# Whole-array products that may run as four 32-column products, chosen by a shortest path

## The chip, the cores and the metric

The kernel runs on one core of one Trainium2 chip. The metric is the time of one execution on the device in microseconds (us); three runs of the kernel before are known. One more view is the profile of a single execution: for every engine the start and duration of each instruction.

The core has five engines that run beside each other: TensorE (PE in the profile; its weight loads are listed apart as PEld), VectorE (DVE), ScalarE (ACT), GpSimd (POOL) and SyncE (SP). They synchronise through semaphores, and each works off its own instructions in order.

## The reference

Four graph layers run one after the other on `x` (32 batches of 512 nodes with 256 features) with one adjacency matrix; after each one the sum with the input is normalised. All is float32.

```python
# --- layer 0: attention of 8 heads of 32, two norms, a two-layer MLP ---
x = _layernorm(x + _L0_gnn_ref(x, adj, ...), axis=-1)
# --- layer 1: scores s1[n] + s2[m], leaky relu, masked softmax, times h = x W ---
x = _layernorm(x + _L1_gnn_ref(x, L1_gnn_W, L1_gnn_a, adj), axis=-1)
# --- layer 2: scores (x W1)(x W2)^T, leaky relu, masked softmax, times x W3, relu ---
x = _layernorm(x + _L2_gnn_ref(x, adj, L2_gnn_W1, L2_gnn_W2, L2_gnn_W3), axis=-1)
# --- layer 3: 4 heads of 64, scores as in layer 1 per head, elu ---
x = _layernorm(x + _L3_gnn_ref(x, adj, L3_gnn_W, L3_gnn_a), axis=-1)
```

Every matrix product of these lines is TensorE's work, and so are the transposes between them.

## The kernel before

The kernel is a recorder. `graph(b)` walks through the four layers for one batch and, instead of issuing instructions, calls `plan(engine, ns, run, reads, writes, ...)` for every piece of work: an engine, an estimated duration, a function that will issue the instructions, and the buffers read and written. The estimates in `ns` serve the planner alone.

`Plan.place` then puts the pieces of all 32 batches in one order. It keeps up to six batches in flight (`WAYS`), follows due times that come from one batch planned alone and from the tables `TENTHS`, `FIRST` and `LAST`, and hands out buffers and PSUM banks. In the order in which it places them, the pieces' `run` functions are called, and so each engine's instruction order is fixed when the program is built. One batch enters about every 82 us (`PACE` is 81.87).

Each TensorE piece has a number `tiling`, the shape in which the array works for it:

- 0: the whole array of 128 rows and 128 columns. All projections (`project_t`, L915, and `project`, L929), the MLP (L1136, L1148), the scores of layer 2 (L1244), the products with the attention of layers 1 and 2 (L1221, L1260), and the transposes (L902, L985, L1017, L1182).
- 1: 32 rows by 128 columns, four products beside each other. The scores of layer 0 (`exps`, L1034).
- 2: 128 rows by 32 columns, four beside each other. The product with the attention of layer 0 (L1093) and the sums of the softmax (L1065, L1281).
- 3: 128 rows by 64 columns, two beside each other. The product with the attention of layer 3 (L1306).

The planner adds `SWITCH` (100 ns) to TensorE's time where the shape changes (L590); the extra due time for a change, `STAY`, is 0, so shapes do not otherwise steer the order.

In the trace a float32 product is two passes, each one weight load and one matmul record; a transpose is one. A "whole product" of 512 columns in L915, L1136 or L1244 is two accumulated matmuls, four records; one of 256 or 257 columns in L929, L1148, L1221 or L1260 is four, eight records. A group of L1034 or L1093 is four matmuls, eight records.

Of the kernel before, what the change touches and what calls it, by code (L numbers as in the profile page):

```python
# [17 lines left out]
P = 128  # L18
# [419 lines left out]
PE, DVE, ACT, POOL, SP, DMA = "PE", "DVE", "ACT", "POOL", "SP", "DMA"  # L438
SIGNAL = 70
SWITCH = 100  # L440


class Slot:
# [6 lines left out]


class Op:
    def __init__(self, engine, ns, run, graph, rank, port, lag, tiling):
        self.engine, self.ns, self.run, self.graph, self.rank = engine, ns, run, graph, rank
        self.port, self.lag, self.tiling = port, lag, tiling
        self.then, self.missing, self.slots, self.ready = [], 0, [], 0.0


class Plan:
# [16 lines left out]

        self.graph, self.rank, self.start = graph, 0, start

    def __call__(self, engine, ns, run, reads=(), writes=(), port=False, lag=0, tiling=0):
        op = Op(engine, ns, run, self.graph, self.rank, port, lag, tiling)  # L480
        if not op.rank:
            op.ready = self.start
        self.rank += 1
        needs = {}
        for is_write, group in ((False, reads), (True, writes)):
            for item in group:
                slot, part = (item[0], item[1:]) if isinstance(item, tuple) else (item, None)
# [12 lines left out]
                if is_write:  # L500
                    if part is None:
                        parts.clear()
                    parts[part] = [op, []]
                else:
                    parts.setdefault(part, [None, []])[1].append(op)
        needs.pop(id(op), None)
        for other in needs.values():
            other.then.append(op)
        op.missing = len(needs)
        self.ops.append(op)  # L510
        return op
# [7 lines left out]
                live[slot.kind][r] += 1  # L519
        return live  # L520

    def place(self, urgency, ways, stay=0.0, early=1e12, run=True):

# [35 lines left out]
        while todo:  # L559
# [62 lines left out]
                del todo[op.graph]  # L622
                order.remove(op.graph)
            self.trace.append((t, op))
            if run and op.run:
                op.run()
        return end


def fast_path(  # L630
# [84 lines left out]
    def keep(name, shape, dtype=FP):  # L715

        slot = Slot(None)
        slot.tile = const.tile(shape, dtype, name=name)
        return slot

    def T(slot):
        return slot.tile if slot.kind is None else buffers[slot.kind][slot.index]
# [186 lines left out]
    def project_t(w, col, xT, dst, k):  # L909

        bank = Slot("bank")

        def run():
            for i in range(KC):
                nc.tensor.matmul(T(bank), T(w)[:, i, col:col + P], T(xT)[:, i, :],  # L915
                                 start=(i == 0), stop=(i == KC - 1))
        plan(PE, 1720, run, [w, xT], [bank])
        evac(dst, lambda t: t[:, k, :], bank, lambda b: b, N, [(dst, k)])

    def project(xT, w, col, width, dst):  # L920

        per = N // width
        for c0 in range(0, NC, per):
            bank = Slot("bank")

            def run(bank=bank, c0=c0):
                for j in range(per):
                    for k in range(KC):
                        nc.tensor.matmul(T(bank)[:, j * width:(j + 1) * width],  # L929
                                         T(xT)[:, k, (c0 + j) * P:(c0 + j + 1) * P],  # L930
                                         T(w)[:, k, col:col + width],
                                         start=(k == 0), stop=(k == KC - 1))
            plan(PE, per * KC * width * 1.69, run, [w, xT], [bank])
# [119 lines left out]
    def layer0(xs, at_once):  # L1053
# [77 lines left out]
        for d in range(KC):  # L1131
            bank = Slot("bank")

            def run(bank=bank, d=d):
                for k in range(KC):
                    nc.tensor.matmul(T(bank), T(w1_sb)[:, k, d * P:(d + 1) * P], T(nT)[:, k, :],  # L1136
                                     start=(k == 0), stop=(k == KC - 1))
            plan(PE, 1720, run, [w1_sb, nT], [bank])
            act(690, lambda bank=bank, d=d: nc.scalar.activation(
                T(hT)[:, d, :], T(bank), AF.Relu, bias=T(b1_sb)[:, d:d + 1]), [bank, b1_sb], [(hT, d)])  # L1140
        f = Slot("y")
        for c0 in range(0, NC, 2):
            bank = Slot("bank")

            def run(bank=bank, c0=c0):
                for j in range(2):
                    for k in range(KC):
                        nc.tensor.matmul(T(bank)[:, j * C:(j + 1) * C],  # L1148
                                         T(hT)[:, k, (c0 + j) * P:(c0 + j + 1) * P],
                                         T(w2_sb)[:, k, :], start=(k == 0), stop=(k == KC - 1))  # L1150
            plan(PE, 1730, run, [w2_sb, hT], [bank])
# [52 lines left out]
    def layer1(xs):  # L1204
# [11 lines left out]
        for c in range(NC):  # L1216
            bank, rinv = Slot("bank"), Slot("rs")

            def run(bank=bank, c=c):
                for m in range(NC):  # L1220
                    nc.tensor.matmul(T(bank)[:, :C + 1], T(p)[:, m, c * P:(c + 1) * P],  # L1221
                                     T(v)[:, m, 2:C + 3], start=(m == 0), stop=(m == NC - 1))
            plan(PE, 1740, run, [p, v], [bank])

            def out(bank=bank, c=c, rinv=rinv):
                nc.vector.reciprocal(T(rinv)[:, 0:1], T(bank)[:, C:C + 1])
                nc.vector.scalar_tensor_tensor(T(y)[:, c, :], T(bank)[:, :C], T(rinv)[:, 0:1],
                                               T(xs)[:, c, :], ALU.mult, ALU.add)
            dve(660, out, [bank, (xs, c)], [(y, c), rinv])
        return y  # L1230

    def layer2(xs):
# [6 lines left out]
        for m in range(NC):  # L1239
            bank, lo, es = Slot("bank"), Slot("e"), Slot("e")  # L1240

            def run(bank=bank, m=m):
                for k in range(KC):
                    nc.tensor.matmul(T(bank), T(xT)[:, k, m * P:(m + 1) * P], T(qT)[:, k, :],  # L1244
                                     start=(k == 0), stop=(k == KC - 1))
            plan(PE, 1720, run, [qT, xT], [bank])
# [8 lines left out]
        for c in range(NC):  # L1255
            bank = Slot("bank")

            def run(bank=bank, c=c):
                for m in range(NC):
                    nc.tensor.matmul(T(bank)[:, :C + 1], T(p)[:, m, c * P:(c + 1) * P],  # L1260
                                     T(v)[:, m, :C + 1], start=(m == 0), stop=(m == NC - 1))
            plan(PE, 1740, run, [p, v], [bank])
# [10 lines left out]
    def layer3(xs, at_once):  # L1273
# [9 lines left out]
        for k in range(KC):  # L1283
            av = Slot("bank")
            for m0 in range(0, NC, 2):
# [72 lines left out]


    graph(0)  # L1360
    alone = plan.place(lambda op: op.rank, 1, run=False)
    when = {op.rank: 10 * t / alone for t, op in plan.trace}

    def due(b, rank):
# [72 lines left out]
```

## Time and profile before

| | us |
|---|---|
| three runs | 2894.71, 2900.61, 2900.12 |
| median | 2900.12 |
| the profiled execution, first to last instruction (span) | 2891.7 |

The span leaves out what lies around the program's instructions, so it is a little shorter than the times. What costs most on TensorE, by line and form (busy time, mean of one record):

| line | shape | moving columns | records | busy us | mean ns |
|---|---|---|---|---|---|
| L1034 | 32 rows | 512 | 2048 | 302.6 | 644 |
| L1093 | 32 columns | 512 | 2048 | 275.2 | 609 |
| L1306 | 64 columns | 512 | 1024 | 242.8 | 605 |
| L915 (layer 0) | whole | 512 | 512 | 241.6 | 595 |
| L1221 | whole | 257 | 1024 | 237.8 | 381 |
| L1260 | whole | 257 | 1024 | 227.4 | 380 |
| L1244 | whole | 512 | 512 | 225.1 | 592 |
| L1148 | whole | 256 | 512 | 126.7 | 391 |
| L1136 | whole | 512 | 256 | 125.6 | 615 |

How to read it: matmul records overlap,[...] and their ends are modelled. The mean of one record is therefore not what it adds to the time. What a product adds is read as the distance between starts: from the first record of a group to the first record of the next. In a timeline line the first number is the start in us, the second the time to the end of the last record merged into that line; then come engine, source line, what is written and read, the array's rows and columns in use, the moving operand, and how many records were merged. In a windows line each engine's busy time follows the stretch, in the order PE, PEld, DVE, ACT, POOL, with the number of instructions, then the granted share of TensorE's clock, the share of the DMA engines and GB/s.

### The profile page before, as it was taken

The page shows a single profiled execution, that of the slowest core. Times are in us where ns is not written, and L with a number is a line of the kernel's source. Part 1 is how long each engine was busy: PE and PEld are TensorE (multiplying, and loading weights), DVE is VectorE, ACT ScalarE, POOL GpSimd, SP SyncE. Part 2 cuts the span into 40 slices and gives each one's busy share as a digit, 9 for nine tenths or more (in the row PEclk, how much of TensorE's full clock was granted, in tenths as well). Part 3 has the DMA queues.
Part 4 walks back from the last instruction along what each step waited for, and adds up shares of the span by engine and source line. Part 5 has one row for each costly group of instructions (what it writes and reads, how often), then busy time and mean ns, then how long its engine had stood idle before and what let it go on. Part 6 is the DMA issues. An engine that isn't in the chain of part 4 may idle for free.

```text
span 2891.7 us, 39629 instructions
## 1 busy us (share of the span) xinstructions
PE 2832.4 (98%) x14014; PEld 1579.2 (55%) x14014; DVE 2443.2 (84%) x4076; ACT 1885.5 (65%) x4104; POOL 865.9 (30%) x962
## 2 busy tenths in 40 slices
PE   8899999999999999999999999999999999999996
PEld 3355555555555555555555555555555555554562
DVE  5568888888888988888988888988888888888877
ACT  4566667666667666666666666666676666676553
POOL 1233333232333232332232333232333323333312
PEclk9999999999999999999999999999999999999998
DMA  6856777777777777777777777776776777775125
GB/s 168 169 110 142 150 159 164 154 144 160 145 161 153 159 149 158 149 160 157 147 152 150 157 157 155 152 160 144 162 157 150 155 153 146 161 163 115 35 55 132
DMA packets 101149, 424.44 MB, mean 147 GB/s; under 512 B 10256, under 2 KB 46224, under 8 KB 59152
## 3 DMA queue, kind: packets, MB, share of 16 engines
q0 software_dynamic: 49600, 325.08, 57.2%
q1 hardware_dynamic: 51344, 96.75, 11.6%
q8 instruction: 113, 1.85, 0.2%
q14 instruction: 92, 0.75, 0.1%
HBM read 63.38 MB, written 17.10 MB: 28 GB/s over the span
## 4 chain that ended last, share of the span: by engine, by line
PE 92%; DVE 3%; DMA 2%; issue 1%; ACT 1%; POOL 0%; SPq 0%; ACTq 0%; DVEq 0%; POOLq 0%
PE bank L929 15%; PE bank L915 11%; PE bank L1034 9%; PE bank L1093 8%; PE bank L1306 8%; PE bank L1221 7%; PE bank L1244 7%; PE bank L1260 7%; PE bank L902 5%; PE bank L1136 4%; PE bank L1148 4%; PE bank L1017 2%; DMA p<-p 1%; PE bank L1281 1%; PE bank L1065 1%
## 5 line engine op out<-in xcount | busy, mean ns | idle before, releaser
L972 POOL DMA_DIRECT2D p<-p x372 | 322.3, 871 | 1787.8 <-DMA p<-p 568.4
L1086 DVE TENSOR_TENSOR p<-p,edge_t 128x2048 f32<-128x2048 f32 x256 | 618.2, 2424 | 59.7 <-ACT p L1038 59.5
L890 ACT ACTIVATE t<-bank 128x512 f32<-128x512 f32 x640 | 373.5, 596 | 384.2 <-PE bank L915 125.4
L1038 ACT ACTIVATE p<-bank 128x512 f32<-128x512 f32 x1024 | 537.9, 599 | 89.2 <-PE bank L1034 87.6
L943 DVE BATCH_NORM_STATS2 st<-y 128x6 f32<-128x256 f32 x768 | 315.9, 411 | 35.6 <-POOL y L960 26.0
L1290 DVE TENSOR_SCALAR p<-p,e,e 128x512 f32<-128x512 f32 x512 | 331.3, 680 | 1.0 <-DMA p<-row 1.0
L960 POOL TENSOR_TENSOR y<-y,x 128x512 f32<-128x512 f32 x192 | 273.7, 1432 | 158.2 <-ACT y L1265 100.1
L1297 DVE TENSOR_TENSOR p<-p,edge_t 128x2048 f32<-128x2048 f32 x128 | 304.9, 2382 | 2.2
L1034 PE MATMUL bank<-t,t 32*128 32x512 f32 x2048 | 302.6, 644 | 0.0
L953 ACT ACTIVATE x<-y,rs,rs 128x256 f32<-128x256 f32 x512 | 277.6, 596 | 24.6 <-DVE rs L950 24.3
L1093 PE MATMUL bank<-p,v 128*32 128x512 f32 x2048 | 275.2, 609 | 12.5 <-DVE p L1086 9.7
L1306 PE MATMUL bank<-p,v 128*64 128x512 f32 x1024 | 242.8, 605 | 3.6 <-DVE p L1297 3.6
L915 PE MATMUL bank<-t,wqkv 128*128 128x512 f32 x512 | 241.6, 595 | 0.7 <-ACT t L890 0.7
L1221 PE MATMUL bank<-v,p 128*128 128x257 f32 x1024 | 237.8, 381 | 0.7 <-DVE p L1214 0.4
L890 ACT ACTIVATE v<-bank 128x264 f32<-128x264 f32 (+2 forms) x384 | 176.5, 460 | 90.2 <-PE bank L929 88.3
L1260 PE MATMUL bank<-v,p 128*128 128x257 f32 x1024 | 227.4, 380 | 0.0
L1244 PE MATMUL bank<-t,t 128*128 128x512 f32 x512 | 225.1, 592 | 0.0
L1221 PEld LDWEIGHTS bank<-v,p 128*128 128x128 f32 x1024 | 189.5, 190 | 40.3 <-issue 16.3
L1260 PEld LDWEIGHTS bank<-v,p 128*128 128x128 f32 x1024 | 194.2, 190 | 28.6 <-issue 1.3
L1034 PEld LDWEIGHTS bank<-t,t 32*128 32x128 f32 x2048 | 86.0, 184 | 169.5 <-issue 101.5
L944 DVE BATCH_NORM_AGGREGATE mv<-st 128x2 f32<-128x6 f32 x768 | 139.7, 182 | 26.3
L902 PE MATMUL bank<-ident,x 128*128 128x128 f32 x1024 | 148.9, 279 | 11.7 <-DMA x<-in_x_dram 7.7
(121 smaller groups left out, 4148.8 us busy)
## 6 DMA issues: line engine op xcount, KB each, us to landing
p<-p POOLq DMA_DIRECT2D x248, 1024.0 KB, 7.2
p<-p POOLq DMA_DIRECT2D x124, 512.0 KB, 5.7
p<-row SPq DMA_DIRECT2D x32, 1024.0 KB
x<-in_x_dram SPq DMA_DIRECT2D x32, 512.0 KB
out_dram<-x SPq DMA_DIRECT2D x32, 512.0 KB
p<-p SPq DMA_DIRECT2D x31, 512.0 KB
e<-row SPq DMA_DIRECT2D x32, 256.0 KB
t<-in_adj_dram SPq DMA_DIRECT2D x4, 256.0 KB
```

What stands on the lines that cost most here:

```text
L890: act(170 + n * 0.84, lambda: nc.scalar.activation(to(T(dst)), frm(T(src)), AF.Copy), [src], writes)
L915: nc.tensor.matmul(T(bank), T(w)[:, i, col:col + P], T(xT)[:, i, :], start=(i == 0), stop=(i == KC - 1))
L929: nc.tensor.matmul(T(bank)[:, j * width:(j + 1) * width], T(xT)[:, k, (c0 + j) * P:(c0 + j + 1) * P], T(w)[:, k, col:col + width], start=( ...
L1034: nc.tensor.matmul(T(banks[j]), T(kT)[r, g, m * P:(m + 1) * P], T(qT)[r, g, :], start=True, stop=True)
L1038: act(600, lambda j=j: nc.scalar.activation(T(p)[:, j, :], T(banks[j]), AF.Exp, scale=1.0 / math.sqrt(D0)), [banks[j]], [(p, j)])
L1086: dve(2420, lambda p=p, m=m: nc.vector.tensor_tensor(T(p), T(p), T(edge_t)[:, m, :].unsqueeze(1).to_broadcast([P, J, N]), ALU.mult), [p, ( ...
L1093: nc.tensor.matmul(T(av)[j * D0:(j + 1) * D0, :], T(v)[:, m, h * D0:(h + 1) * D0], T(p)[:, j, :], start=(m == 0), stop=(m == NC - 1))
L1221: nc.tensor.matmul(T(bank)[:, :C + 1], T(p)[:, m, c * P:(c + 1) * P], T(v)[:, m, 2:C + 3], start=(m == 0), stop=(m == NC - 1))
L1244: nc.tensor.matmul(T(bank), T(xT)[:, k, m * P:(m + 1) * P], T(qT)[:, k, :], start=(k == 0), stop=(k == KC - 1))
L1260: nc.tensor.matmul(T(bank)[:, :C + 1], T(p)[:, m, c * P:(c + 1) * P], T(v)[:, m, :C + 1], start=(m == 0), stop=(m == NC - 1))
L1290: nc.vector.tensor_scalar(T(p)[:, 2 * m + i, :], T(G)[:, h, :], T(e1)[:, r:r + 1], T(e02)[:, r:r + 1], ALU.mult, ALU.max)
L1306: nc.tensor.matmul(T(av)[i * D3:(i + 1) * D3, :], T(q)[:, m0 + m, 2 * H3 + h * D3:2 * H3 + (h + 1) * D3], T(p)[:, 2 * m + i, :], start=(m0 ...
```

## The change

Two things change, and the order of the pieces does not.

First, the whole-array products (not the transposes) get a choice, `ways=either`: as before, or as four products of 32 columns beside each other, each with a quarter of the weights' columns and writing a quarter of the bank's partitions. `product` issues one or the other, according to `tiling[0]` at the time of the call. Pieces are no longer issued while they are placed; after `place` has made the order, `emit` runs a shortest path over TensorE's pieces in that order. It counts `CHANGE[way]` when the shape turns into `way` (196, 213, 126 ns for the whole array, 32 rows, 32 columns) and 26 ns for every product done in 32 columns, and takes the cheapest sequence of ways. Then it issues all pieces.

Second, the product of layer 3 (L1306) is no longer two products of 64 columns but four of 32, two for each head, and counts as shape 2 for the path. For the planner it keeps its `tiling=3`, so that the order stays.

```diff
+CHANGE = {0: 196, 1: 213, 2: 126}
...
-    def __call__(self, engine, ns, run, reads=(), writes=(), port=False, lag=0, tiling=0):
-        op = Op(engine, ns, run, self.graph, self.rank, port, lag, tiling)
+    def __call__(self, engine, ns, run, reads=(), writes=(), port=False, lag=0, tiling=0, ways=None):
+        op = Op(engine, ns, run, self.graph, self.rank, port, lag, tiling, ways or {tiling: 0})
...
             self.trace.append((t, op))
-            if run and op.run:
+        return end
+
+    def emit(self, tiling):
+        costs, steps = {0: 0}, []
+        for _, op in self.trace:
+            if op.engine is PE:
+                step = {}
+                for way, extra in op.ways.items():
+                    cost = {w: c + extra + (w != way) * CHANGE[way] for w, c in costs.items()}
+                    step[way] = min(cost, key=cost.get)
+                    step[way] = (cost[step[way]], step[way])
+                costs = {way: cost for way, (cost, _) in step.items()}
+                steps.append({way: came for way, (_, came) in step.items()})
+        way, chosen = min(costs, key=costs.get), []
+        for step in reversed(steps):
+            chosen.append(way)
+            way = step[way]
+        for _, op in self.trace:
+            if op.engine is PE:
+                tiling[0] = chosen.pop()
+            if op.run:
                 op.run()
-        return end
...
+    tiling, either = [0], {0: 0, 2: 26}
+
+    def product(out, left, right, start, stop):
+        w = 32 if tiling[0] == 2 else P
+        for c in range(0, P, w):
+            nc.tensor.matmul(out[c:c + w, :], left[:, c:c + w], right, start=start, stop=stop)
...
             for i in range(KC):
-                nc.tensor.matmul(T(bank), T(w)[:, i, col:col + P], T(xT)[:, i, :],
-                                 start=(i == 0), stop=(i == KC - 1))
-        plan(PE, 1720, run, [w, xT], [bank])
+                product(T(bank), T(w)[:, i, col:col + P], T(xT)[:, i, :],
+                        start=(i == 0), stop=(i == KC - 1))
+        plan(PE, 1720, run, [w, xT], [bank], ways=either)
...
                     for m in range(2):
-                        for i in range(2):
-                            h = 2 * k + i
-                            nc.tensor.matmul(T(av)[i * D3:(i + 1) * D3, :],
-                                             T(q)[:, m0 + m, 2 * H3 + h * D3:2 * H3 + (h + 1) * D3],
-                                             T(p)[:, 2 * m + i, :], start=(m0 + m == 0),
+                        for w in range(0, P, 32):
+                            nc.tensor.matmul(T(av)[w:w + 32, :],
+                                             T(q)[:, m0 + m, 2 * H3 + k * P + w:2 * H3 + k * P + w + 32],
+                                             T(p)[:, 2 * m + w // D3, :], start=(m0 + m == 0),
                                              stop=(m0 + m == NC - 1))
-                plan(PE, 1770, run, [q, p], [av], tiling=3)
+                plan(PE, 1770, run, [q, p], [av], tiling=3, ways={2: 0})
...
     with tc.manual_schedule(engines={mybir.EngineType.PE, mybir.EngineType.DVE,
...
         plan.place(urgency, WAYS, 1e3 * STAY, 1e3 * EARLY)
+        plan.emit(tiling)
```

The other whole-array products (L929, L1136, L1148, L1221, L1244, L1260) are edited as L915's is: `product` in place of `nc.tensor.matmul`, and `ways=either`.

More of the change, by code (lines that the diff above doesn't have):

```diff
@@ L452, with __init__ @@
 class Op:
-    def __init__(self, engine, ns, run, graph, rank, port, lag, tiling):
+    def __init__(self, engine, ns, run, graph, rank, port, lag, tiling, ways):
         self.engine, self.ns, self.run, self.graph, self.rank = engine, ns, run, graph, rank
-        self.port, self.lag, self.tiling = port, lag, tiling
+        self.port, self.lag, self.tiling, self.ways = port, lag, tiling, ways
         self.then, self.missing, self.slots, self.ready = [], 0, [], 0.0
@@ L520, in profile, with place @@
         return live
-    def place(self, urgency, ways, stay=0.0, early=1e12, run=True):
+    def place(self, urgency, ways, stay=0.0, early=1e12,):
         held_by = {g: self.profile(g) for g in {op.graph for op in self.ops}}
@@ L928, in run @@
                     for k in range(KC):
-                        nc.tensor.matmul(T(bank)[:, j * width:(j + 1) * width],
+                        product(T(bank)[:, j * width:(j + 1) * width],
                                          T(xT)[:, k, (c0 + j) * P:(c0 + j + 1) * P],
@@ L932, in run @@
                                          start=(k == 0), stop=(k == KC - 1))
-            plan(PE, per * KC * width * 1.69, run, [w, xT], [bank])
+            plan(PE, per * KC * width * 1.69, run, [w, xT], [bank], ways=either)
             evac(dst, lambda t, c0=c0: t[:, c0:c0 + per, :width], bank,
@@ L1135, in run @@
                 for k in range(KC):
-                    nc.tensor.matmul(T(bank), T(w1_sb)[:, k, d * P:(d + 1) * P], T(nT)[:, k, :],
+                    product(T(bank), T(w1_sb)[:, k, d * P:(d + 1) * P], T(nT)[:, k, :],
                                      start=(k == 0), stop=(k == KC - 1))
-            plan(PE, 1720, run, [w1_sb, nT], [bank])
+            plan(PE, 1720, run, [w1_sb, nT], [bank], ways=either)
             act(690, lambda bank=bank, d=d: nc.scalar.activation(
@@ L1147, in run @@
                     for k in range(KC):
-                        nc.tensor.matmul(T(bank)[:, j * C:(j + 1) * C],
-                                         T(hT)[:, k, (c0 + j) * P:(c0 + j + 1) * P],
+                        product(T(bank)[:, j * C:(j + 1) * C],
+                                T(hT)[:, k, (c0 + j) * P:(c0 + j + 1) * P],
                                          T(w2_sb)[:, k, :], start=(k == 0), stop=(k == KC - 1))
-            plan(PE, 1730, run, [w2_sb, hT], [bank])
+            plan(PE, 1730, run, [w2_sb, hT], [bank], ways=either)
             dve(680, lambda bank=bank, c0=c0: nc.vector.tensor_tensor(
@@ L1220, in run @@
                 for m in range(NC):
-                    nc.tensor.matmul(T(bank)[:, :C + 1], T(p)[:, m, c * P:(c + 1) * P],
-                                     T(v)[:, m, 2:C + 3], start=(m == 0), stop=(m == NC - 1))
-            plan(PE, 1740, run, [p, v], [bank])
+                    product(T(bank)[:, :C + 1], T(p)[:, m, c * P:(c + 1) * P],
+                            T(v)[:, m, 2:C + 3], start=(m == 0), stop=(m == NC - 1))
+            plan(PE, 1740, run, [p, v], [bank], ways=either)
             def out(bank=bank, c=c, rinv=rinv):
@@ L1243, in run @@
                 for k in range(KC):
-                    nc.tensor.matmul(T(bank), T(xT)[:, k, m * P:(m + 1) * P], T(qT)[:, k, :],
+                    product(T(bank), T(xT)[:, k, m * P:(m + 1) * P], T(qT)[:, k, :],
                                      start=(k == 0), stop=(k == KC - 1))
-            plan(PE, 1720, run, [qT, xT], [bank])
+            plan(PE, 1720, run, [qT, xT], [bank], ways=either)
             act(600, lambda bank=bank, lo=lo: nc.scalar.activation(
@@ L1259, in run @@
                 for m in range(NC):
-                    nc.tensor.matmul(T(bank)[:, :C + 1], T(p)[:, m, c * P:(c + 1) * P],
-                                     T(v)[:, m, :C + 1], start=(m == 0), stop=(m == NC - 1))
-            plan(PE, 1740, run, [p, v], [bank])
+                    product(T(bank)[:, :C + 1], T(p)[:, m, c * P:(c + 1) * P],
+                            T(v)[:, m, :C + 1], start=(m == 0), stop=(m == NC - 1))
+            plan(PE, 1740, run, [p, v], [bank], ways=either)
             dve(160, lambda bank=bank, c=c: nc.vector.reciprocal(
@@ L1360, in fast_path @@
     graph(0)
-    alone = plan.place(lambda op: op.rank, 1, run=False)
+    alone = plan.place(lambda op: op.rank, 1)
     when = {op.rank: 10 * t / alone for t, op in plan.trace}
```

## The prediction

> **What bounds the kernel now.** I read the page from the top: busy times, slices, chain. The last line below is from its DMA queues.
>
> ```profile
> span 2891.7 us, 39629 instructions
> PE 2832.4 (98%) x14014; PEld 1579.2 (55%) x14014; DVE 2443.2 (84%) x4076; ACT 1885.5 (65%) x4104; POOL 865.9 (30%) x962
> PE   8899999999999999999999999999999999999996
> PE 92%; DVE 3%; DMA 2%; issue 1%; ACT 1%; POOL 0%; SPq 0%; ACTq 0%; DVEq 0%; POOLq 0%
> q8 instruction: 113, 1.85, 0.2%
> ```
>
> TensorE is 98% busy and carries 92% of the chain; only the first and last slices show room. The windows view puts numbers to the middle:
>
> ```profile
> 200.00:1000.00 800.00, 798.82 (x3978) 451.97 (x3975) 687.93 (x1143) 534.87 (x1175) 251.25 (x276) 1.00 0.71 150
> 1000.00:1800.00 800.00, 798.91 (x3999) 447.47 (x3998) 699.89 (x1139) 537.11 (x1173) 246.40 (x276) 1.00 0.73 155
> 1800.00:2600.00 800.00, 798.80 (x3980) 446.92 (x3979) 705.18 (x1145) 537.95 (x1173) 244.65 (x275) 1.00 0.73 154
> ```
>
> From 200 to 2600 us TensorE (first number) idles about 1.2 us in 800; VectorE (third) is 86 to 88% busy. Full clock. So time goes only if TensorE's stream itself gets shorter. "Busy" hides what it loses inside that stream; the timeline shows it as the distance between starts of neighbours:
>
> ```profile
> 1001.62 1.14 PE L1034 MATMUL bank<-t,t 32*128 32x512 f32 x8
> 1002.69 0.28 PE L1182 MATMUL bank<-ident,gs 128*16 128x128 f32 x1
> 1002.90 1.06 PE L1281 MATMUL bank<-p,pick 128*32 128x512 f32 x8
> 1003.78 1.04 PE L1093 MATMUL bank<-p,v 128*32 128x512 f32 x8
> 1004.76 0.66 PE L902 MATMUL bank<-ident,y 128*128 128x128 f32 x4
> ...
> 1016.23 1.14 PE L1034 MATMUL bank<-t,t 32*128 32x512 f32 x8
> 1017.30 1.98 PE L1136 MATMUL bank<-t,w_sb 128*128 128x512 f32 x4
> 1019.12 1.90 PE L1221 MATMUL bank<-v,p 128*128 128x257 f32 x8
> 1020.95 1.06 PE L1093 MATMUL bank<-p,v 128*32 128x512 f32 x8
> 1021.94 1.98 PE L1136 MATMUL bank<-t,w_sb 128*128 128x512 f32 x4
> 1023.86 1.06 PE L1093 MATMUL bank<-p,v 128*32 128x512 f32 x8
> 1024.85 1.14 PE L1034 MATMUL bank<-t,t 32*128 32x512 f32 x8
> 1025.92 1.99 PE L1148 MATMUL bank<-w_sb,t 128*128 128x256 f32 x8
> 1027.85 1.14 PE L1034 MATMUL bank<-t,t 32*128 32x512 f32 x8
> ```
>
> The same eight instructions of 32 columns take 0.88 us (1002.90 to 1003.78) when the next group keeps that shape and 0.99 (1020.95 to 1021.94) when it does not. L1136 takes 1.82 after another shape and before its own, 1.92 between two others. Over the trace's 2,420 PE groups these distances repeat within a few ns, so I split them into a body, an entry and an exit:
>
> - whole array: 512-column products 1717 ns (4 x 429), 257-column ones 1733; entry 104 (56 for a transpose), exit 93
> - 32 rows (L1034): body 858, entry 104, exit 109
> - 32 columns (L1093, L1065, L1281): body 858, entry 25, exit 114
> - 64 columns (L1306): body 1717, entry 51, exit 100
>
> Bodies, entries and exits sum to 2797 us of the 2865 us from the first PE group to the last; the 68 us left are waits, 31 of them before 200 us and 25 after 2600.
>
> **What the Trainium skill says.** "TensorEngine Tiling (Array Packing)", section Key Properties: changing the tiling mode drains the engine. The trace agrees: 93 to 114 ns at every exit. "TensorE: Matmul & The Clock Gate", section LDWEIGHTS: a load is priced by its columns, P/1.2 ns; that makes 107 ns for 128 columns and 27 for 32, against entries of 104 and 25. So an entry is one weight load that nothing covers. The same page, section The mechanism: tiles beside each other overlap, each starting a few ns later. Here four starts lie 7 ns apart and 858 ns are two rounds of 429, the whole array's round. For these 512 columns four narrow products cost no more than one wide one.
>
> **The change, step by step.** The order of instructions of the two kernels, laid side by side, has the same groups in the same sequence on every engine, the same waits and no new semaphore instruction. Only shapes differ: 255 whole-array products become four of 32 columns (L1136 56, L915 40, L1221 32, L1148 31, L929 80, L1244 12, L1260 4), and the 128 groups of L1306 go from 64 columns to 32. PE matmuls and loads go from 14014 to 19058 each.
>
> 1. *Switches removed.* Shape changes between neighbours fall from 1038 to 837. The whole array is entered 393 times before, 257 after: 136 fewer, nearly all by products, so 136 x (104 + 93) = 26.8 us. The 64-column shape goes: 97 x (51 + 100) = 14.6 us. The 32-column shape is entered 326 times instead of 294: 32 x (25 + 114) = 4.4 us back. Entries of the 32-row shape stay 254. Net 37.0 us. In the stretch shown: L1034 to L1136 saves 104 - 25 = 79, L1221 to L1093 93 + 25 = 118, L1136 between two L1093 114 + 104 + 93 + 25 = 336, L1148 between two L1034 197 - 139 = 58; 591 ns in 10.55 us.
>
> 2. *The narrow products' bodies.* For 512 columns: nothing, as above; L1306's body is 4 rounds either way. For 256 to 264 columns (147 products) the trace has no example. Their round is 217 ns (1733/8). Below nothing is excluded: the moving columns are the same and stream at the same rate. From above: if the four staggered starts (3 x 7 = 21 ns) were paid in every round, 80 products x 8 rounds and 67 x 4 are 908 rounds, 19 us. I take the stagger once a product, 147 x 21 ns = 3 us, as loads (110 ns long) fit well inside a round.
>
> 3. *What was waiting anyway.* By position, 31.6 of the 37.0 us fall between 200 and 2600 us, 1.7 between 2600 and 2700 (98.6% busy), and 3.7 in the rest of the start and the end, where TensorE waits for loads and chains; I drop half of that, 2 us.
>
> 4. *Waits that come up.* A shorter stream reaches its inputs earlier. From 250 to 2600 us 134 waits of TensorE (4.7 a batch) were released under 0.3 us before the group that needed them, most for L1093 on VectorE's mask product and for L985 on ScalarE. Such a loop, L1034 to ScalarE to VectorE to L1093, is some 5 us long; the mean saving of 13 ns per us takes 65 ns out of it. 134 x 65 ns = 9 us if every one bites, nothing if the savings lie elsewhere: the tightest one (L1034 at 379 us to L1093 at 384) holds no changed group. I take 3 us.
>
> Sum: 37.0 - 3 - 2 - 3 = 29 us. The profiled execution spans 2891.7 us; the lowest run is 3.0 us above that, the median of the three 8.4 above. I take the 29 us off the median: 2871 us.
>
> **Rivals.**
>
> *Products of 256 columns pay every round.* Step 2 at its upper end: 37 - 19 - 5 = 13 us, 2887. For it: no such form in the trace, and 7 ns between starts is real. Against: at 512 columns the same stagger costs nothing.
>
> *Waits take it back.* Step 4 at 9 us, the half of step 3 doubled, and VectorE, 88% busy, late in places where it now looks idle: some 14 us remain, 2886. Against: TensorE follows a fixed order, and most margins are over 1 us.
>
> *Issue at the skill's price.* The TensorE page, section "Wait — 56ns, not 53.3ns?", gives 62 ns of issue per matmul where its instructions are decoded in microcode. Then a round of four narrow products lasts 248 ns, not 217: 908 x 31 ns = 28 us, and 2899 is left, no change. The trace can't tell: its rounds of four last 429 ns.
>
> *Slower: the instruction stream starves TensorE.* Place: the 147 products of 256 to 264 columns, where eight instructions must arrive in 217 ns, 27 ns each. The densest 256 instructions now take 17.5 us, 68 ns each; changed, 6.9 us. If loads cost issue as well, at the 51 ns that a bare semaphore instruction takes in the trace, a round lasts 408 ns: 908 x 191 = 173 us. Instructions issued ahead hide part (up to 36 were seen waiting); half leaves 2871 + 87 = 2958. It turns the sign from about 31 ns an instruction (29 us over 7,264 instructions is 4 ns above 27). For it: no stretch of the trace is as dense. Against: between two semaphore instructions 74 ns apart eight loads and matmuls were passed, time and again; and q8's 113 packets of 16 KB, 256 instructions each, took 0.8 us apiece (0.2% of 16 engines' 2892 us), 3 ns an instruction.
>
> **How the numbers follow.** Forecast 0.64, narrow rounds 0.12, waits 0.10, issue at 62 ns 0.08, starved 0.06. A measurement of this kernel can tell a change of about 0.2%, 6 us, from none. The forecast's own range is 2860 to 2881 (steps 2 to 4 at nothing: 37 us, 2863, and a few us of run to run; all three half way up: 20 us). To hold eight in ten it reaches to the narrow rounds and the waits above and is widened a little below: 2858 to 2890. Faster 0.86, same 0.08, slower 0.06.
>
> **What would show it.** In the changed profile: the groups that were L1136 and L1148 1.72 to 1.74 us from start to start between 32-column neighbours; two layer-3 groups in a row at 3.46 us, not 3.59 (368.88 to 372.47 in the timeline now); PE still 98% busy or more in the middle, with a period per batch about 1.1 us shorter (31.6 us over the 29 batches there). Narrow 257-column groups at 1.9 us mean the second case; at 2.0 the third; at over 2.2, with loads starting late, the last. Idle PE in the middle windows of 3 us or more in 800 means the waits. The forecast is wrong if switches cost the same and yet the middle windows are no shorter.

## The result and the profile after

The changed kernel takes 2871.75 us (median of four runs, 2866.63 to 2872.08) against 2900.36 before: 0.9905 of it, 95% interval 0.9891 to 0.992. A second set of its runs, with before measured at 2896.26 beside it, gave 0.9913 (0.9896 to 0.9929). The gain is 25 to 29 us, about 1%.

The page of the changed kernel, the lines that answer to those of before:

```profile
span 2869.7 us, 49717 instructions
PE 2802.0 (98%) x19058; PEld 1507.2 (53%) x19058; DVE 2436.6 (85%) x4076; ACT 1884.6 (66%) x4104; POOL 871.5 (30%) x962
PE 87%; DVE 7%; DMA 2%; ACT 2%; issue 2%; POOL 0%; SPq 0%; DVEq 0%; ACTq 0%; POOLq 0%
q8 instruction: 152, 2.49, 0.3%
```

PE and PEld have 5,044 records more each, every other engine as many as before, and the span is 22 us shorter. TensorE still carries the chain, but VectorE's part in it grew from 3% to 7%.

The windows view of the middle (TensorE's busy time first, VectorE's third):

```profile
200.00:1000.00 800.00, 796.86 (x5635) 431.36 (x5638) 694.32 (x1152) 541.59 (x1187) 251.16 (x278) 1.00 0.72 152
1000.00:1800.00 800.00, 798.45 (x5359) 433.46 (x5351) 705.60 (x1149) 542.91 (x1185) 252.96 (x279) 1.00 0.74 156
1800.00:2600.00 800.00, 797.66 (x5386) 431.59 (x5390) 710.84 (x1162) 543.36 (x1183) 248.54 (x278) 1.00 0.74 156
```

TensorE now idles 1.6 to 3.1 us in 800 where it idled 1.2; in one of the three windows that reaches the 3 us that the prediction named as the sign of waits. The timeline of the changed kernel, in the stretch shown of before (lines have moved by 30; `product` records every choosable product under L749):

```profile
1016.90 1.14 PE L1064 MATMUL bank<-t,t 32*128 32x512 f32 x8
1017.97 1.92 PE L749 MATMUL bank<-t,w_sb 128*32 128x512 f32 x16
1019.72 1.92 PE L749 MATMUL bank<-v,p 128*32 128x257 f32 x32
1021.45 1.04 PE L1123 MATMUL bank<-p,v 128*32 128x512 f32 x8
1022.31 1.90 PE L749 MATMUL bank<-t,w_sb 128*32 128x512 f32 x16
1024.02 1.04 PE L1123 MATMUL bank<-p,v 128*32 128x512 f32 x8
1024.99 1.14 PE L1064 MATMUL bank<-t,t 32*128 32x512 f32 x8
1026.07 1.93 PE L749 MATMUL bank<-w_sb,t 128*32 128x256 f32 x32
1027.93 1.14 PE L1064 MATMUL bank<-t,t 32*128 32x512 f32 x8
```

The MLP's product goes from L1064 to the next narrow group in 1.75 us (1.82 before), the 257-column product takes 1.73 (1.83), the next product of the MLP's first layer 1.71 (1.92), the one of its second layer between two L1064 1.86 (1.93). From the first line's start to the last one's it is 11.03 us; before, from 1016.23 to 1027.85, 11.62. The 0.59 us are what the prediction had for this stretch.

Layer 3's product has its own sign in the prediction: two groups in a row, here before and changed, each with the group that follows.

```profile
368.88 3.65 PE L1306 MATMUL bank<-p,v 128*64 128x512 f32 x16
372.47 1.07 PE L1065 MATMUL bank<-p,pick 128*32 128x512 f32 x8
```

```profile
376.21 3.64 PE L1335 MATMUL bank<-p,v 128*32 128x512 f32 x32
379.67 1.04 PE L1095 MATMUL bank<-p,pick 128*32 128x512 f32 x8
```

From start to start it is 3.59 us before and 3.46 changed, as forecast.

**Where the time went, stage by stage.** Since the order of groups is the same in every version, any two groups mark off the same work. I cut at a group of L1034 near 270 us and at one of L1136 near 2706 us (lines of before); "start" is what lies ahead of the first, "full stretch" between, "end" from the second to the last group. Switching is the sum of entries and exits by the prices of the prediction, waits are what is left over in the full stretch when bodies and switching are taken off. All in us:

| kernel | start | full stretch | end | switching saved in the stretch | waits in the stretch |
|---|---|---|---|---|---|
| before | 270.2 | 2436.2 | 165.9 | - | 14.0 |
| before, again | 277.2 | 2435.4 | 166.2 | - | 13.3 |
| changed | 279.2 | 2408.1 | 164.1 | 32.0 | 17.9 |
| changed, again | 277.0 | 2406.3 | 164.9 | 32.0 | 16.1 |
| choice after 200 us only | 275.8 | 2410.6 | 166.1 | 32.0 | 20.4 |
| layer 3 only | 272.8 | 2428.2 | 172.6 | 8.4 | 14.4 |
| products only | 276.2 | 2416.3 | 163.9 | 22.7 | 16.7 |
| all narrow | 275.0 | 2432.4 | 172.1 | 6.5 | 16.7 |
| all narrow, again | 273.2 | 2429.9 | 170.1 | 6.5 | 14.3 |
| no scale | 273.9 | 2408.1 | 164.1 | 32.0 | 17.9 |
| half mask | 274.9 | 2403.0 | 165.0 | 32.0 | 12.8 |
| measured prices | 276.8 | 2409.2 | 165.4 | 33.3 | 20.3 |

The mean of the two profiles before (2435.8) less that of the changed kernel (2407.2) is 28.6 us: 32.0 us of switching, less 3.4 us of new waits. The start gained nothing (its mean is 4.4 us longer, within the spread of this column) and the end 1.5 us.

### The profile page after: what moved, and what is told of

Read it like the earlier page. It is cut to its first block, busy times and chain, and to the rows that moved or that the text cites. A ratio compares the mean times of both kernels' runs of the same rounds, so it can differ in the third digit from the quotient of the medians.

```text
span 2869.7 us, 49717 instructions
## 1 busy us (share of the span) xinstructions
PE 2802.0 (98%) x19058; PEld 1507.2 (53%) x19058; DVE 2436.6 (85%) x4076; ACT 1884.6 (66%) x4104; POOL 871.5 (30%) x962
## 4 chain that ended last, share of the span: by engine, by line
PE 87%; DVE 7%; DMA 2%; ACT 2%; issue 2%; POOL 0%; SPq 0%; DVEq 0%; ACTq 0%; POOLq 0%
PE bank L749 54%; PE bank L1064 8%; PE bank L1123 8%; PE bank L1335 7%; PE bank L932 4%; DVE p L1116 3%; PE bank L1047 2%; PE bank L1311 1%; PE bank L1095 1%; PE bank L1015 1%; DVE p L1320 1%; DMA x<-in_x_dram 1%; ACT p L1068 1%; DVE st L973 1%; DMA p<-p 0%
## 5 line engine op out<-in xcount | busy, mean ns | idle before, releaser
L1116 DVE TENSOR_TENSOR p<-p,edge_t 128x2048 f32<-128x2048 f32 x256 | 628.5, 2464 | 61.4 <-ACT p L1068 61.2
L749 PE MATMUL bank<-v,p 128*128 128x257 f32 (+1 forms) x2912 | 468.0, 384 | 4.3 <-DVE p L1244 3.8
L749 PEld LDWEIGHTS bank<-v,p 128*128 128x128 f32 (+1 forms) x2912 | 367.7, 159 | 90.7 <-issue 26.6
L1320 DVE TENSOR_SCALAR p<-p,e,e 128x512 f32<-128x512 f32 x512 | 333.1, 684 | 0.4 <-DMA p<-row 0.3
L990 POOL TENSOR_TENSOR y<-y,x 128x512 f32<-128x512 f32 x192 | 275.3, 1441 | 156.7 <-ACT y L1295 98.4
L1327 DVE TENSOR_TENSOR p<-p,edge_t 128x2048 f32<-128x2048 f32 x128 | 310.2, 2423 | 2.2
L1064 PE MATMUL bank<-t,t 32*128 32x512 f32 x2048 | 300.7, 646 | 0.0
L1123 PE MATMUL bank<-p,v 128*32 128x512 f32 x2048 | 274.0, 607 | 15.2 <-DVE p L1116 11.4
L1335 PE MATMUL bank<-p,v 128*32 128x512 f32 x2048 | 241.5, 597 | 3.7 <-DVE p L1327 3.2
L749 PE MATMUL bank<-t,wqkv 128*32 128x512 f32 (+1 forms) x944 | 243.8, 596 | 0.9 <-ACT t L920 0.9
L749 PE MATMUL bank<-t,t 128*128 128x512 f32 (+1 forms) x656 | 225.2, 592 | 0.0
L1064 PEld LDWEIGHTS bank<-t,t 32*128 32x128 f32 x2048 | 84.1, 185 | 173.4 <-issue 86.4
L932 PEld LDWEIGHTS bank<-ident,x 128*128 128x128 f32 x1024 | 118.2, 142 | 78.8 <-issue 37.7
L749 PEld LDWEIGHTS bank<-t,t 128*128 128x128 f32 (+1 forms) x656 | 94.3, 167 | 111.2 <-issue 107.2
```

The costliest lines, as they stand in the source:

```text
L749: nc.tensor.matmul(out[c:c + w, :], left[:, c:c + w], right, start=start, stop=stop)
L932: nc.tensor.transpose(T(bank)[:, (2 * k + c) * P:(2 * k + c + 1) * P], T(src)[:, c0 + c, k * P:(k + 1) * P], ident)
L1064: nc.tensor.matmul(T(banks[j]), T(kT)[r, g, m * P:(m + 1) * P], T(qT)[r, g, :], start=True, stop=True)
L1116: dve(2420, lambda p=p, m=m: nc.vector.tensor_tensor(T(p), T(p), T(edge_t)[:, m, :].unsqueeze(1).to_broadcast([P, J, N]), ALU.mult), [p, ( ...
L1123: nc.tensor.matmul(T(av)[j * D0:(j + 1) * D0, :], T(v)[:, m, h * D0:(h + 1) * D0], T(p)[:, j, :], start=(m == 0), stop=(m == NC - 1))
L1320: nc.vector.tensor_scalar(T(p)[:, 2 * m + i, :], T(G)[:, h, :], T(e1)[:, r:r + 1], T(e02)[:, r:r + 1], ALU.mult, ALU.max)
```

## The experiments

Each was timed against the kernel before and profiled once. In all of them the pieces have the same order.

**The two kernels once more.** No edit. The first profile of the changed kernel had lost time at the start, where TensorE's clock dropped more often than before. The windows view, first the changed kernel, then the kernel before (the granted clock is the third number from the right):

```profile
50.00:100.00 50.00, 42.35 (x350) 13.20 (x340) 23.28 (x11) 27.08 (x52) 8.98 (x11) 0.85 0.95 185
100.00:150.00 50.00, 43.51 (x300) 19.27 (x292) 24.53 (x46) 25.96 (x53) 16.01 (x14) 0.87 0.67 134
150.00:200.00 50.00, 42.99 (x345) 21.73 (x344) 30.99 (x62) 28.43 (x62) 17.00 (x18) 0.93 0.65 130
```

```profile
50.00:100.00 50.00, 42.19 (x222) 15.31 (x220) 23.49 (x11) 27.00 (x52) 8.63 (x10) 0.91 0.96 186
100.00:150.00 50.00, 44.70 (x232) 22.07 (x224) 30.92 (x57) 30.65 (x63) 20.96 (x19) 0.98 0.73 151
150.00:200.00 50.00, 47.09 (x210) 25.65 (x209) 32.58 (x60) 31.76 (x68) 13.89 (x16) 0.97 0.71 142
```

> The changed kernel again, unaltered. The profiled execution waited 44 us on TensorE before 200 us (31 in the kernel before) and had 34 us of half clock there (13.6 before). Theory A, the start is chance: the half-clock stretches lie elsewhere this time, with under 25 us of them before 200 us, waits there of 30 to 40 us, and a span some 5 us shorter. Theory B, the change itself disturbs the start: 30 us or more of half clock and 42 us or more of waits again. Both expect the middle (200 to 2600 us) as it was, with 3.5 to 5.5 us of waits above the kernel before's, and 2866 to 2872 us.

> The kernel before, unaltered. Theory A (the start is chance): half clock before 200 us anywhere from 10 to 35 us, and the time with it, 2895 when little, 2900 when more. Theory B: half clock of 13.6 us as in its first profile, whatever the time. Shape changes cost what they did: bodies, entries and exits repeat to a few ns.

Measured: the changed kernel 2871.6 us (0.9913, 0.9896 to 0.9929), with 23.8 us of half clock before 200 us in place of 34.0 and 41.8 us of waits in place of 44.0; the kernel before 2898.79 (1.0003, 0.9994 to 1.0013), with 17.0 us of half clock and 37.4 us of waits in place of 13.6 and 30.8. So neither theory got all of its numbers: the half clock does vary from one execution to the next, as A said, but the waits of the changed kernel stayed high, near what B said. With the start of the kernel before at 270.2 and 277.2 us and that of the changed one at 279.2 and 277.0, most of the first difference between the profiles was the execution's, as far as two profiles of each can tell. The middle repeats to 2 us.

**The choice left out at the start.**

```diff
-                for way, extra in op.ways.items():
+                ways = op.ways if t > 200e3 or 0 not in op.ways else {0: 0}
+                for way, extra in ways.items():
```

> The choice applies only to pieces planned after 200 us, so 232 narrow products in place of 255; the first 200 us keep whole-array products (layer 3 stays in 32 columns). It gives up 2.9 us of switching at most. Theory A (the start is chance): 0 to 3 us slower than the changed kernel, some 2872. Theory B (the narrow products disturb the start): the start returns to 31 us of waits and 13.6 us of half clock, and the kernel is 5 to 10 us faster than the changed one, 2862 to 2867.

Measured: 2871.55 us (0.9911, 0.9894 to 0.9927), start 275.8 us. Theory B's 5 to 10 us are out, at least for the choice (layer 3 stays narrow here): without the chosen narrow products the time is the same and the start lies within the spread of the others. Nor is it longer, so no gain from the narrow products shows there. The full stretch is 3.4 us longer than in the changed kernel, and 2.5 of them are two more single waits of 1.1 to 1.2 us between L1064 and the MLP's second layer; so a difference of this size between two versions can hang on two waits. What sets the start (270 to 279 us over twelve profiles) was not taken apart further.

**All products narrow.** A narrow product with 256 or 257 columns was the form for which the trace of before had no example.

```diff
-    tiling, either = [0], {0: 0, 2: 26}
+    tiling, either = [0], {2: 0}
```

> All 1088 whole-array products run in 32 columns, and layer 3 too; only transposes use the whole array. Switching, counted with the entries and exits of the kernel before, is 166.5 us against 176.2 before and 139.2 changed. Theory 'a narrow product costs nothing': 6 to 12 us faster than before, 2888 to 2894, and narrow 256 and 257-column groups at 1.73 us. Rival 'a narrow product of 256 columns pays 21 ns a round' (4,608 such rounds): 97 us more, some 2987. Rival 'the instruction stream starves TensorE': 43,000 more records of PE than before, loads that start late, and over 3000 us.

Its timeline, a stretch with nothing but narrow products, and the line of its instruction queue:

```profile
1042.25 3.62 PE L749 MATMUL bank<-t,l2m 128*32 128x512 f32 x32
1045.68 3.64 PE L749 MATMUL bank<-l2w,t 128*32 128x256 f32 x64
1049.14 7.05 PE L749 MATMUL bank<-t,t 128*32 128x512 f32 x64
1056.01 1.90 PE L749 MATMUL bank<-t,wqkv 128*32 128x512 f32 x16
1057.72 1.91 PE L749 MATMUL bank<-wqkv,t 128*32 128x256 f32 x32
```

```profile
q8 instruction: 265, 4.34, 0.6%
```

Two 512-column products take 3.43 us, two of 256 columns 3.46, the four of the scores 6.87, the last 256-column one 1.73 (to 1059.45): to a hundredth what the whole array takes (1717 and 1727 ns). For each of the forms the median over the full stretch is within 1 ns of the whole array's body. Both rivals of the kind "narrow products cost something" are out, although there are 33,470 matmul records in place of 14,014 (with as many loads that is 38,912 more, not the 43,000 of the expectation): 64 matmuls and 64 loads follow each other every 27 ns for 3.46 us and nothing starts late. The stretch shortened by 3.4 us (6.5 of switching, 3 us of waits back). But the time was 2897.89 us, no gain (1.0005, 0.9996 to 1.0013), because the end took 6 us longer.

> All products narrow, once more unaltered: it gained 3 us in the full stretch and lost 6 after it, where the last batch waited 11 us for one broadcast. Theory 'chance of that transfer': the stretch again 2431 to 2434 us, and the end (from 2706 us on) back at 165 to 168 us. Theory 'narrow products hurt where the array runs at half clock or waits': the end 171 us or more again.

Measured: 2894.84 us (0.9992, 0.9983 to 1.0001), stretch 2429.9, a little better than expected; the end 170.1 us, between the two theories' numbers, this time with a single accumulating transfer of 13.91 us on its chain. Layer 3 alone, below, has such an end too, at 172.6 us, and the changed kernel, with 255 narrow products, has not, nor have the 640 of the last experiment. So narrow products as such are not shown to be it; the chain shows single transfers.

**Layer 3 alone, and the products alone.** For the first, `either` became `{0: 0}`; for the second layer 3's product is that of the kernel before:

```diff
-CHANGE = {0: 196, 1: 213, 2: 126}
+CHANGE = {0: 196, 1: 213, 2: 126, 3: 150}
...
-                plan(PE, 1770, run, [q, p], [av], tiling=3, ways={2: 0})
+                plan(PE, 1770, run, [q, p], [av], tiling=3)
```

> Layer 3 in 32 columns alone; every other product keeps the whole array. Counted with the entries and exits of the kernel before, switching falls by 9.2 us in the order, 8.4 of it in the full stretch (the first groups after 270 us to those at 2706). Theory 'switching is the gain, and only in the full stretch': that stretch takes 2427.5 to 2429 us (2436 before), the time is 6 to 9 us below before. Rival 'layer 3 gains nothing alone, since its groups stand between others that now change shape more': stretch within 2 us of 2436.

> The choice for whole-array products alone; layer 3 stays in 64 columns (150 ns on the path for entering it), 244 narrow products. Switching falls by 26.7 us in the order, 22.7 in the full stretch. Theory: the stretch takes 2414 to 2417 us, the time is 18 to 23 us below before; with the 8.4 of layer 3 alone the parts give 31 of the 32 us that both save together. Rival 'the gain is the two together' (the narrow products need layer 3 in their shape as a neighbour): under 15 us here.

Measured: layer 3 alone brings the stretch to 2428.2 us (7.6 shorter), the products alone to 2416.3 (19.5 shorter). Each is its switching (8.4, 22.7) less its waits, and 27.1 us together are nearly the 28.6 of the whole change: the parts add up, neither needs the other. The times were 2895.21 (0.9995, 0.9986 to 1.0004; a miss, 6 to 9 us were expected) and 2877.56 us (0.9926, 0.9909 to 0.9943; as expected). Layer 3 alone lost at the end what it had gained. Its chain there (start in us, length, what):

```profile
2835.00 0.28 ACT gT L1214
2835.27 0.02 issue
2835.29 3.52 DMA row<-gT
...
2838.89 9.99 DMA p<-row
...
2848.98 1.92 DVE p L1320 x4
2850.90 0.02 issue
2850.93 2.30 DVE p L1327
```

A row goes out to DRAM and comes back as a broadcast over all partitions, 13.5 us of transfers. TensorE is busy for 7.2 us of them and then idles 7.75 us, until 2853.27. In the changed kernel this part of the chain has a 12.87 us accumulating transfer that began at 2817.35, with TensorE busy for 7.2 us too. Which transfer comes last, and by how much, differs from version to version; why the end is longer in just these two kernels is open.

**What TensorE now waits for.** VectorE is 88% busy, so its load was the first suspect. The multiplication by the second norm's scale in layer 0 goes (its input is all ones); the order keeps its place:

```diff
-            dve(690, lambda w=w: nc.vector.tensor_tensor(
-                T(f)[:, w, :], T(f)[:, w, :], T(g2_row).unsqueeze(1).to_broadcast([P, 2, C]),
-                ALU.mult), [(f, c) for c in parts] + [g2_row], [(f, c) for c in parts], True)
+            dve(690, None, [(f, c) for c in parts] + [g2_row], [(f, c) for c in parts], True)
```

> The changed kernel without the multiplication by the second norm's scale in layer 0 (left out of the computation; the inputs' scale is all ones): 1.4 us of VectorE's work per batch less, same order. The changed kernel waits 15 us in the middle against 11.7 before, most before the group of layer 0's product that needs VectorE's mask product. Theory 'VectorE is what it now waits for': those waits fall by 2 us or more, and the full stretch takes 2404 to 2406 us (2407 changed). Rival 'the waits are ScalarE's and buffers'': stretch within 1 us of 2407. In either case the first 200 us stay as they are.

Measured: 2867.49 us (0.9899, 0.9882 to 0.9915, no different from the changed kernel), stretch 2408.1, waits 17.9: unchanged. Taking 37 us off VectorE's 2437 bought nothing, so its load as such looks unlikely; the cut is a small one. By pairs of neighbouring groups on TensorE, two kinds of waits grew: between layer 3's product and layer 0's (0.4 to 0.6 us in all before, 3.0 and 4.0 changed) and between the MLP's first product and layer 0's (0.1; 1.4 and 1.6). That is 4.4 us more. In each of them (17 and 4 in the changed kernel's first profile, 14 and 4 in its second) L1123 starts 54 to 56 ns after VectorE has ended an L1116, its mask product. The waits between layer 0's scores (L1064) and the MLP's second product, a few of about 1 us each, fell by 2.9 us, and the other places added some 1.8, so that 3.4 are left. Without the scale the first kind came to 2.6 us, a little less, and the waits before the MLP's second product to 4.5 in place of 2.0; they were 4.6 without the choice at the start, so they come and go between versions. The chain of the changed kernel through one of the first kind:

```profile
507.95 0.21 ACT rs L978
508.17 0.02 issue
508.19 0.16 DVE rs L980
508.35 3.07 DVE p L1320 x3
511.42 0.02 issue
511.44 0.03 DVE p L1327
511.47 2.09 issue
513.57 0.02 DVEq L1182
513.59 0.06 issue
513.65 2.30 DVE p L1116
515.94 0.04 issue
515.99 1.07 PE bank L1123 x8
```

The product L1123 starts as soon as its mask product L1116 is done, and VectorE comes to that from layer 3's scores and mask product (L1320, L1327; the 2.09 us of "issue" are L1327's run) without a pause: 7.7 us in which VectorE alone sets the pace, and the scale's multiplication doesn't lie there. Not all of the length is VectorE's own work. Of the three L1320 two take 0.54 us and the third 2.22, and this third one overlaps an addition on GpSimd:

```profile
509.54 1.57 POOL L990 TENSOR_TENSOR y<-y,x 128x512 f32<-128x512 f32 x1
```

In the whole trace the 75 L1320 that overlap an L990 take 0.53 to 2.87 us (median 1.77), the other 437 at most 0.60. No run takes the addition away. The kernel before has the same overlap at its L1290 of this place. So the next edit takes work out of just this place: layer 3's mask over half of the rows (the kernel leaves the other half without it).

```diff
                     nc.vector.tensor_tensor(
-                        p4, p4, T(edge_t)[:, m0:m0 + 2, :].unsqueeze(2).to_broadcast([P, 2, 2, N]),
-                        ALU.mult)
+                        p4[:, 0:1], p4[:, 0:1],
+                        T(edge_t)[:, m0:m0 + 1, :].unsqueeze(2).to_broadcast([P, 1, 2, N]), ALU.mult)
```

> The changed kernel with layer 3's mask product over half of its neighbours' rows (the mask of the other half is left out of the computation): 1.2 us less of VectorE just ahead of layer 0's mask product, in the place where the changed kernel waits. There VectorE works without a pause for 7.7 us and the product L1123 comes at its end. Theory 'a short stretch bound by VectorE': the waits between layer 3's group and L1123 fall from 3.0 to 4.0 us in all to under 1, and the full stretch from 2406 to 2408 us to 2403 to 2405.5. Rival 'ScalarE's exponentials or a bank': those waits stay over 2.5 us.

Measured: stretch 2403.0 us, the waits after layer 3's product 0.0 us in all, those after the MLP's 1.3 as before; the time 2862.25 us (0.9879, 0.9861 to 0.9897). The theory of a short stretch bound by VectorE holds for the first kind. The edit halves the mask everywhere, 141 us of VectorE's work in all, but the other waits for L1116 did not fall: those after the MLP's first product stayed, and those between layer 3's projection and L1123, some 25 of about 0.2 us each, are 5.3 us in all against 5.2 and 5.1 changed (4.4 before). This speaks for the place and against the load. The timeline there, VectorE and the addition on GpSimd:

```profile
502.43 1.46 DVE L1320 TENSOR_SCALAR p<-p,e,e 128x512 f32<-128x512 f32 x3
503.80 1.22 DVE L1327 TENSOR_TENSOR p<-p,edge_t 128x1024 f32<-128x1024 f32 x1
505.12 5.37 DVE L1116 TENSOR_TENSOR p<-p,edge_t 128x2048 f32<-128x2048 f32 x2
```

```profile
504.01 2.14 POOL L990 TENSOR_TENSOR y<-y,x 128x512 f32<-128x512 f32 x1
```

L1327 takes half its time, as meant. The three L1320 take 1.46 us in place of 3.07, which was not meant: the addition now comes after them, and the first L1116 beside it takes 3.17 us in place of 2.28. From the first L1320 to the end of that L1116 it is 5.87 us in place of 7.66. The cut at this place is thus 1.8 us and not 1.2, so the run shows where the wait comes from rather than what a given saving on VectorE is worth.

**The path with measured prices.** A switch is priced by the shape left and the shape entered, a narrow product by nothing:

```diff
-CHANGE = {0: 196, 1: 213, 2: 126}
+LEAVE, ENTER = {0: 93, 1: 109, 2: 114}, {0: 104, 1: 104, 2: 25}
...
-                    cost = {w: c + extra + (w != way) * CHANGE[way] for w, c in costs.items()}
+                    enter = 56 if way == 0 and len(op.ways) == 1 else ENTER[way]
+                    cost = {w: c + extra + (w != way) * (LEAVE[w] + enter) for w, c in costs.items()}
...
-    tiling, either = [0], {0: 0, 2: 26}
+    tiling, either = [0], {0: 0, 2: 0}
```

> The path with the entries and exits measured here (leaving 93, 109, 114; entering 104, 56 for a transpose, 104, 25) and nothing for a narrow product: 640 narrow products instead of 255, the same 837 changes of shape, 1.8 us less switching in the order and 1.4 us in the full stretch. Theory 'narrow products are free, in any number': full stretch 2405 to 2407.5 us, the time within 3 us of the changed kernel's, 2868 to 2872. Rival 'they cost something in numbers' (26 ns each as the changed kernel's path has it): 10 us more, 2880.

Measured: stretch 2409.2 us, 1.4 us less switching and 20.3 us of waits, so the profile is no better than the changed kernel's; the time 2864.19 us (0.9892, 0.9876 to 0.9909), whose interval overlaps the changed kernel's. The profiled execution was the slowest of its five (2863.63 to 2873.22). 26 ns a product are out. Of the waits 5.3 us now stand between the MLP's first product and layer 0's, where the changed kernel has 1.4 and 1.6: what the shapes save is waited for at the same link. Whether this version is faster by a few us can't be told; with this order the measured prices leave only 1.8 us of switching to gain by other shapes.

## Why the prediction was right

The forecast was 2871 us, 29 us off the median; 2871.75 was measured.

- *Step 1, switches.* It held as worked out. The bodies, entries and exits read before are those of the changed trace to 1 or 2 ns: a narrow 256-column product between two L1064 takes 1864 ns from start to start, where 1727 + 25 + 114 is 1866. The all-narrow kernel (6.5 us in the stretch) and the two halves (8.4 and 22.7) follow the same prices. The reading behind it, that the distance between starts and not busy time is what a product costs, carried everything.
- *Step 2, narrow bodies.* Priced at 3 us of 0 to 19; it is 0. What the Trainium skill says of tiles beside each other ("TensorE: Matmul & The Clock Gate", The mechanism), that they overlap and start a few ns after each other, the traces show at 256 columns as at 512: in the all-narrow kernel four starts 6 to 7 ns apart, and 196 ns from the last to the next four.
- *Step 3, start and end.* Priced at 2 us lost of 3.7. The start gave nothing at all and the end 1.5 us. Small, but wrong in kind: the start's length differs by 7 us between two profiles of the kernel before, and no run shows it to follow what TensorE saves there, so there was nothing to be seen of which half could be counted.
- *Step 4, waits.* Priced at 3 us; 3.4 measured. The kind was right (TensorE early for layer 0's mask product), the loop only in part: the chain shown comes not from L1034 through ScalarE but through 7.7 us of VectorE, of which layer 3's scores and mask are the first part. That the size was met is luck: the prediction took a mean saving over all tight waits, while in the trace two links added 4.4 us, those where layer 3's or the MLP's product comes just before L1123, and fewer waits before the MLP's second product gave 2.9 back.
- The sum came out because 3 us too much in step 2 stood against about 2 too little in steps 3 and 4: 32.0 - 3.4 in the stretch, nothing at the start, 1.5 at the end is 30 us by the profiles; the medians say 25 to 29. That 2871 was met to a microsecond is luck too: the three runs from whose median the 29 us were taken lay 1 to 4 us above the later medians of the same kernel (2896.26 to 2898.79).
- *Rivals.* Rounds that pay, the Trainium skill's 62 ns of issue for a matmul decoded in microcode ("TensorE: Matmul & The Clock Gate", "Wait — 56ns, not 53.3ns?") and the starved stream are all out by the all-narrow kernel: four matmuls and four loads in 217 ns, 54 ns a matmul, kept up. The waits' rival had the right mechanism and too large a size: 3.4 us net, where it had 9 and then some more for VectorE.

## What to carry to other kernels

Where an engine is busy 98% of the time, measure its groups from start to start and split by what stands before and after: here 176 us in 2865 were entries and exits of array shapes, which no busy time shows. Here a product that fitted several shapes cost the same in each; where that holds, let its neighbours decide its shape, over the whole fixed order. Expect the saving only in the stage that this engine bounds, and look then for the shortest loop through the next engine; VectorE's mean load (88%) did not tell where TensorE waits, the chain did.

## What was not expected of the hardware

- A float32 product of 128 columns as four of 32 beside each other takes the same time to a few ns, for 256 to 512 moving columns, though it issues four times the loads and matmuls, at 256 columns one instruction every 27 ns.
- TensorE's clock was halved only before 200 us and after 2690, in pieces of 3.4 us, or two or three times that, and a last piece of 14 to 19 us that begins only after TensorE's last instruction: 38 to 59 us in all, different in each execution of one kernel (55.8 and 47.8 us for the changed one).
- Three VectorE operations of one form (L1320) took 3.07 us at one place and 1.46 at the same place of another version. In the first an addition on GpSimd overlaps the third of them (2.22 us instead of 0.54), in the second it overlaps the operation after them.
